# Group-norm chains of a linear-attention and Fourier convolution kernel: four stages on TensorE replaced by two, about a reference mean

## The chip, the cores and the metric

The kernel runs on one core of one Trainium2 chip. The metric is the device time of the whole program in microseconds (us), the median of several executions. The engines are TensorE (PE; its weight loads are listed as PEld), VectorE (DVE), ScalarE (ACT), GpSimd (POOL) and SyncE (SP, which here only issues DMAs). Each takes its instructions in a fixed order; an instruction waits on semaphores for those of other engines and for DMAs.

## What is computed

Two residual layers over an image batch of shape (8, 384, 64, 64), each preceded by a group normalisation over 32 groups of 12 channels:

```python
def _gn(v, G=32, eps=1e-5):
    B_, C_, H_, W_ = v.shape
    g = v.reshape(B_, G, C_ // G, H_, W_)
    m = jnp.mean(g, axis=(2, 3, 4), keepdims=True)
    s = jnp.var(g, axis=(2, 3, 4), keepdims=True)
    return ((g - m) / jnp.sqrt(s + eps)).reshape(v.shape)

x = x + linear_attention(_gn(x), ...)   # 1x1 projections q, k, v, rotary turn, elu+1, output projection
x = x + fourier_conv(_gn(x), ...)       # 1x1 projection, 8x8 block FFT filter, 3x3 depthwise, GELU gate, 1x1 projection
```

## The kernel before

The batch elements b = 0 to 7 are worked one after the other. Channels are three tiles of 128 partitions (`CT = 3`), the 4096 positions are 8 bands of 512 columns (`NBAND`, `BT`). A batch element passes three times: a first pass over its bands makes keys and values (`Keys.project`, lines 455 to 542), a second pass makes queries and adds the attention's output to x (`queries`, lines 1121 to 1181), a third pass does layer 1. The third pass of b is interleaved, band by band, with the first pass of b + 1 (lines 1297 to 1328), and the depthwise sums of b's last two bands are finished inside the second pass of b + 1 (`last_bands`, lines 1244 to 1272).

Everything is issued by one Python program; generators that yield between steps are advanced by hand to set the order on TensorE, and a scheduler of the framework sets the order of the other engines' instructions from the program and its estimates. Tiles come from pools with a fixed number of buffers; the pool "w" has ten, shared by most working tiles.

Statistics. For layer 0 of batch 0, `input_stats` (line 158) runs `bn_stats` on DVE over each band as it lands. For every other normalisation `band_sums` (line 165) accumulates on ACT, band by band, the sum and the sum of squares of each channel about `shift`, minus the mean of the channel's first 64 columns, which DVE makes at band 0 (lines 172 and 173). `mean_and_variance` (line 191) turns either into a mean and a variance for each channel, `mv`.

The chain. `norm_chain` (line 264) takes the channels' `mv` to the groups' mean and inverse deviation and back to the channels. It has four stages on TensorE, each of three `matmul` calls (six instructions in float32):

- `ps_m`: the mean over the group's channels; copied to `gm` (line 291);
- `ps_mc`: that mean sent to the channels; DVE makes each channel's squared difference from it plus its variance, `d` (lines 294 to 298);
- `ps_v`: the mean of `d` over the group; a root on ACT (line 303) and a Newton step on DVE (lines 304 to 310) make `rsg`;
- `ps_r`: `rsg` sent to the channels; `rs` and `nb_` are the scale and the bias of the affine pass `normalised` (line 363, tiles `hf`).

The chain is used nine times: once for layer 0 of batch 0, through `layer0_chain` (line 1020), where `rs` scales the key weights and a third parameter, `shift`, corrects the key bias (`first_k_bias`); and once for layer 1 of each batch, between the second and the third pass. Layer 0 of the batches 1 to 7 uses `far_chain` (line 322) instead, on DVE and POOL's DMAs, inside the second pass. In the layer-1 use the stages stand between other TensorE work: the key projections of the next batch (`pk`, line 490) and the contraction of the last band but one or two (`pw`, lines 946 and 957). How many of these steps come between two stages is set by line 1285:

```python
for steps in (3, 0, 1, 3) if last else (4, 1, 1, 4) if b else (2, 1, 1, 3):
    next(chain)
    for _ in range(steps):
        next(more, None)
run(chain)
```

After the chain come the rest of the key steps, a value projection (`pv`, line 506) and the projection of the first band of layer 1 (`pi`, line 751), which reads `hf`.

The start. As the bands of batch 0 land, TensorE transposes their tokens (`px`, line 452, `turn_tokens`), ACT copies them, DVE takes the statistics; then come the weight sums (`pg_wk`, `pgt_wk`, lines 386 and 391), the chain, the correction of the key bias (`pbk`, line 405), and the key projections.

POOL's queue. In the second pass POOL issues, in this order: the far chain's first two DMAs (lines 329 and 330, `moments`, `of_groups`), the DMAs that add single taps of the depthwise sum to `dw` in place (line 822), the far chain's last four (lines 352 to 358), the bias DMAs (lines 432 and 433), and the outputs (line 978). An instruction that waits there holds all that come after it.

Of the kernel before, what the change touches and what calls it, by code (L numbers as in the profile page):

```python
# [24 lines left out]
NG = 32  # L25
GROUP = C // NG
# [91 lines left out]
def conv_blocks_kernel(ctx: ExitStack, tc: tile.TileContext, a: dict, out: bass.AP, nb: int):  # L118
    nc = tc.nc
# [33 lines left out]
    def line_tile(name):  # L153
        return small.tile([P, C], F32, tag="line", name=name, bufs=1)

    stats, moments = {}, {}

    def input_stats(j):

        if j == 0:  # L160
            stats[0, 0] = w_tile([P, CT, NBAND, 6], "st_0")
        for t in range(CT):
            nc.vector.bn_stats(stats[0, 0][:, t, j, :], xt[0, j][:, t, :])

    def band_sums(b, layer, j, x_, out):


        n = f"{layer}_{b}"
        if j == 0:
            shift = small.tile([P, CT], F32, tag=f"shift{layer}", name=f"shift{n}")  # L170
            sums = small.tile([P, CT, 2, NBAND], F32, tag=f"sums{layer}", name=f"sums{n}", bufs=2 - layer)
            nc.vector.tensor_reduce(shift, x_[:, :, :W], mybir.AxisListType.X, ALU.add)
            nc.vector.tensor_scalar_mul(shift, shift, -1.0 / W)
            moments[b, layer] = shift, sums
        shift, sums = moments[b, layer]
        for m in range(CT):
            of_m = [sums[:, m, i, j : j + 1] for i in range(2)]
            nc.scalar.activation(  # L178
                out[:, m, :], x_[:, m, :], AF.Identity, bias=shift[:, m : m + 1], accum_out=of_m[0]
            )  # L180
            nc.scalar.activation(out[:, m, :], out[:, m, :], AF.Square, accum_out=of_m[1])

    def stream_stats(b, j):

# [3 lines left out]
        nc.sync.dma_start(t, x_in[b][:, :, j * BT : (j + 1) * BT])  # L188
        band_sums(b, 0, j, t, t)

    def mean_and_variance(b, layer):

        mv = small.tile([P, CT, 2], F32, tag="mv", name=f"mv{layer}_{b}")
        if (b, layer) in stats:
            st = stats.pop((b, layer))
            for t in range(CT):
                nc.vector.bn_aggr(mv[:, t, :], st[:, t, :, :].rearrange("p a b -> p (a b)"))
            return mv
# [3 lines left out]
        nc.vector.tensor_scalar_mul(s_[:, :, 0], s_[:, :, 0], 1.0 / N)  # L202
        nc.vector.tensor_sub(mv[:, :, 0], s_[:, :, 0], shift)
        nc.vector.tensor_mul(s_[:, :, 0], s_[:, :, 0], s_[:, :, 0])
        nc.vector.scalar_tensor_tensor(mv[:, :, 1], s_[:, :, 1], 1.0 / N, s_[:, :, 0], ALU.mult, ALU.subtract)
# [29 lines left out]
    def weight(name, queue):  # L235
# [25 lines left out]

    gated = const.tile([P, BT + HT], F32, tag="gated", name="gated")

    def norm_chain(b, layer, params):


        n = f"{layer}_{b}"
        mv = mean_and_variance(b, layer)

        def group_mean(src, name):  # L270
            ps = ps_tile(name)
            for t in range(CT):
                nc.tensor.matmul(
                    ps[:NG, 0:1], to_group[:, t, :], src[:, t : t + 1], start=(t == 0), stop=(t == CT - 1)
                )
            return ps[:NG, 0:1]

        def to_channels(src, name):
            ps = ps_tile(name)
            for m in range(CT):  # L280
                nc.tensor.matmul(
                    ps[:, m : m + 1], of_group[:, m * P : (m + 1) * P], src, start=True, stop=True
                )
            return ps[:, 0:CT]

        def group_tile(name):
            return small.tile([NG, 1], F32, tag=name, name=f"{name}{n}")

        yield
        gm = group_tile("gm")  # L290
        nc.vector.tensor_copy(gm, group_mean(mv[:, :, 0], f"ps_m{n}"))
        yield
        minus_mean = small.tile([P, CT], F32, tag=f"mm{layer}", name=f"mm{n}")
        nc.vector.tensor_scalar_mul(minus_mean, to_channels(gm, f"ps_mc{n}"), -1.0)
        d = small.tile([P, CT], F32, tag="d", name=f"d{n}")
        nc.vector.tensor_add(d, mv[:, :, 0], minus_mean)
        nc.vector.tensor_mul(d, d, d)
        nc.vector.tensor_add(d, d, mv[:, :, 1])
        yield
        var = group_tile("var")  # L300
        nc.vector.tensor_scalar_add(var, group_mean(d, f"ps_v{n}"), 1e-5)
        rsg = group_tile("rsg")
        nc.scalar.activation(rsg, var, AF.Sqrt)
        nc.vector.reciprocal(rsg, rsg)

        y = group_tile("y")
        nc.vector.tensor_mul(y, rsg, rsg)
# [5 lines left out]
        nc.vector.tensor_copy(rs, to_channels(rsg, f"ps_r{n}"))  # L313
        nb_ = small.tile([P, CT], F32, tag=f"nb{layer}", name=f"nb{n}")
        nc.vector.tensor_mul(nb_, minus_mean, rs)
        params += rs, nb_
        if layer == 0:
            shift = group_tile("shift")
            nc.vector.scalar_tensor_tensor(shift, gm, -1.0, rsg, ALU.mult, ALU.mult)
            params.append(shift)  # L320

    def far_chain(b, params):

# [78 lines left out]
    def first_k_bias(params, sums):  # L402

        p_ = ps_tile("pbk_0")
        nc.tensor.matmul(p_[:, :C], params[2].to_broadcast([NG, P]), sums, start=True, stop=True)
# [464 lines left out]
    sums = {}  # L870
# [141 lines left out]
    def layer0_chain(b, prepared):  # L1012

        if b >= nb:
            return
        wk = load_weight(b, "wk", k_runs) if b else first_wk
        params = []
        if b == 0:
            sums = sum_weight(wk, "wk")
            yield from norm_chain(b, 0, params)  # L1020
            scale_weight(wk, params)
            yield
            first_k_bias(params, sums)
            prepared += [params[0], shift_to_all(b, params[2])], wk, kv_bias
# [157 lines left out]

    for j, place in enumerate([None, None, None, "taps", "taps", *ring, None]):
        input_stats(j)
        if j < NBAND - 1:
            transposed[0, j] = xk_tile(0, j, place)
            for i in range(4):
                turn_tokens(0, j, i, transposed[0, j])
# [86 lines left out]
    for b in range(nb):  # L1275
# [136 lines left out]
```

## Time and profile before

| | us |
|---|---|
| median of 3 runs | 3267.61 |
| lowest and highest | 3267.39, 3268.34 |
| the profiled execution | 3267.16 |
| its span on the core | 3265.4 |
| TensorE busy in the span | 3215.4 |
| DVE, ACT, POOL busy | 2622.6, 2155.8, 287.4 |
| first key matmul of batch 0 starts | 32.35 |
| first `pi` of batch 0, 3 and 7 starts | 333.13, 1528.38, 3107.84 |

The profile is one execution, with the start and the duration of each instruction, what ended the idle time before it, and the clock that TensorE was granted. In the views by time a row is: start, duration, engine, line of the kernel, operation, tiles written and read, shapes, count, and in brackets the idle time before it and its releaser. Rows of the same kind in sequence are merged. Matmuls are pipelined, so the time that a group takes from TensorE is read from its start to the start of the next row. A batch's cycle is 398.4 us in the middle of the program.

### The profile page before, as it was taken

The page shows a single profiled execution, that of the slowest core. Times are in us where ns is not written, and L with a number is a line of the kernel's source. Part 1 is how long each engine was busy: PE and PEld are TensorE (multiplying, and loading weights), DVE is VectorE, ACT ScalarE, POOL GpSimd, SP SyncE. Part 2 cuts the span into 40 slices and gives each one's busy share as a digit, 9 for nine tenths or more (in the row PEclk, how much of TensorE's full clock was granted, in tenths as well). Part 3 has the DMA queues.
Part 4 walks back from the last instruction along what each step waited for, and adds up shares of the span by engine and source line. Part 5 has one row for each costly group of instructions (what it writes and reads, how often), then busy time and mean ns, then how long its engine had stood idle before and what let it go on. Part 6 is the DMA issues. An engine that isn't in the chain of part 4 may idle for free.

```text
span 3265.4 us, 53152 instructions
## 1 busy us (share of the span) xinstructions
PE 3215.4 (98%) x21119; PEld 1840.7 (56%) x21119; DVE 2622.6 (80%) x4257; ACT 2155.8 (66%) x4358; POOL 287.4 (9%) x424
## 2 busy tenths in 40 slices
PE   8999999999999999999999999999999999999998
PEld 5544666456664566545665456654566546664455
DVE  6577699886988778896888958988688895988867
ACT  4455666856767566776667766667566674556686
POOL 0000000100001000100001000011000010000065
PEclk9999999999999999999999999999999999999999
DMA  7324243762447524476245652357533573235323
GB/s 221 115 87 112 86 107 99 180 132 86 107 112 175 142 78 100 113 172 150 69 98 134 156 148 66 103 138 153 145 78 98 140 151 99 68 70 131 105 40 59
DMA packets 159484, 377.52 MB, mean 116 GB/s; under 512 B 30372, under 2 KB 41620, under 8 KB 151044
## 3 DMA queue, kind: packets, MB, share of 16 engines
q1 hardware_dynamic: 124500, 282.65, 28.9%
q0 software_dynamic: 34544, 91.26, 17.0%
q8 instruction: 166, 2.72, 0.4%
q14 instruction: 82, 0.67, 0.1%
q10 hardware_dynamic: 192, 0.21, 0.0%
HBM read 235.62 MB, written 99.93 MB: 103 GB/s over the span
## 4 chain that ended last, share of the span: by engine, by line
PE 81%; DVE 10%; ACT 7%; issue 1%; DMA 0%; POOL 0%; SPq 0%; DVEq 0%; ACTq 0%; POOLq 0%
PE pi L751 15%; PE pf L733 14%; PE pk L490 14%; PE pv L506 12%; PE pq L654 8%; PE pw L946 4%; DVE dw L836 4%; PE pd L767 3%; PE pw L957 2%; PE pb L788 2%; PE acc L522 2%; PE acc L535 2%; ACT tap L821 1%; PE pn L692 1%; ACT ring L798 1%
## 5 line engine op out<-in xcount | busy, mean ns | idle before, releaser
L836 DVE SCALAR_TENSOR_TENSOR dw<-ring,w_dw,dw 128x512 f32<-128x512 f32 x1197 | 835.0, 745 | 85.8 <-ACT ring L804 64.8
L490 PE MATMUL pk<-wk,x 128*128 128x384 f32 x1536 | 532.0, 493 | 0.0
L654 PE MATMUL pq<-x,wq 128*128 128x512 f32 x1152 | 512.0, 598 | 11.2 <-DVE qc L666 8.2
L733 PE MATMUL pf<-qc,mt 128*128 128x512 f32 x1152 | 510.2, 596 | 4.5 <-DVE qc L725 4.4
L751 PE MATMUL pi<-w_in,hf 128*128 128x384 f32 x1536 | 506.7, 487 | 4.8 <-ACT ring L798 4.2
L506 PE MATMUL pv<-wv,x 128*128 128x384 f32 x1344 | 461.9, 488 | 0.0
L751 PEld LDWEIGHTS pi<-w_in,hf 128*128 128x128 f32 x1536 | 291.2, 190 | 207.5 <-ACT ring L798 5.0
L490 PEld LDWEIGHTS pk<-wk,x 128*128 128x128 f32 x1536 | 287.6, 191 | 191.5 <-issue 4.5
L733 PEld LDWEIGHTS pf<-qc,mt 128*128 128x128 f32 x1152 | 215.7, 190 | 274.8 <-issue 253.2
L654 PEld LDWEIGHTS pq<-x,wq 128*128 128x128 f32 x1152 | 215.3, 190 | 269.3 <-issue 243.4
L506 PEld LDWEIGHTS pv<-wv,x 128*128 128x128 f32 x1344 | 253.6, 190 | 177.7 <-issue 4.2
L775 DVE TENSOR_TENSOR tf<-pd,filt 128x384 f32<-128x384 f32 x256 | 125.3, 549 | 161.3 <-PE pd L767 161.1
L493 DVE TENSOR_TENSOR kc<-pk,kvbias 128x384 f32<-128x384 f32 x256 | 140.9, 551 | 84.4 <-PE pk L490 84.2
L378 ACT ACTIVATE qs<-qc 128x512 f32<-128x512 f32 (+1 forms) x128 | 106.8, 835 | 148.0 <-DVE qc L683 146.0
L978 POOL DMA_DIRECT2D out_dram<-y x56 | 72.3, 1291 | 1482.0 <-PE pd L767 1046.3
L178 ACT ACTIVATE differences<-x,shift 128x512 f32<-128x512 f32 x192 | 136.9, 713 | 93.6 <-DVE x L737 72.8
L378 ACT ACTIVATE ks<-kc 128x1536 f32<-128x1536 f32 x64 | 95.0, 1484 | 149.8 <-DVE kc L497 149.8
L758 ACT COPY ht<-pi 128x384 f32<-128x384 f32 x256 | 113.4, 477 | 121.0 <-PE pi L751 120.1
L513 ACT COPY v<-pv 128x384 f32<-128x384 f32 x224 | 105.2, 478 | 116.9 <-PE pv L506 114.8
L737 DVE SCALAR_TENSOR_TENSOR x<-pf,bfc,x 128x512 f32<-128x512 f32 x192 | 140.7, 740 | 50.5 <-PE pf L733 49.6
L973 ACT COPY y<-pw 128x512 f32<-128x512 f32 x224 | 90.9, 491 | 128.6 <-PE pw L957 128.6
L946 PE MATMUL pw<-gated,w_out 128*128 128x256 f32 x744 | 172.2, 380 | 0.7 <-DVE tf L775 0.7
(234 smaller groups left out, 4704.2 us busy)
## 6 DMA issues: line engine op xcount, KB each, us to landing
tq<-in_tq SPq DMA_DIRECT2D x64, 1024.0 KB, 7.0
x<-in_x SPq DMA_DIRECT2D x64, 768.0 KB, 4.9
tk<-in_tk SPq DMA_DIRECT2D x64, 768.0 KB, 4.3
out_dram<-x SPq DMA_DIRECT2D x63, 768.0 KB, 6.1
xs<-in_x SPq DMA_DIRECT2D x56, 768.0 KB, 6.2
out_dram<-y POOLq DMA_DIRECT2D x56, 768.0 KB, 8.0
dw<-tap POOLq DMA_DIRECT2D x49, 768.0 KB, 9.8
out_dram<-dw POOLq DMA_DIRECT2D x7, 768.0 KB, 7.5
```

Of the source, the lines that this page charges most:

```text
L178: nc.scalar.activation(out[:, m, :], x_[:, m, :], AF.Identity, bias=shift[:, m : m + 1], accum_out=of_m[0])
L378: nc.scalar.activation(e, x_, AF.Relu, scale=-1.0)
L490: nc.tensor.matmul(pk[:, :C], tokens(t), wks[:, t, :], start=(t == 0), stop=(t == CT - 1))
L493: nc.vector.tensor_add(kc[:, i, :], pk[:, :C], bias)
L506: nc.tensor.matmul(pv[:, :C], xt[b, j][:, t, i * P : (i + 1) * P], wvs[:, t, :], start=(t == 0), stop=(t == CT - 1),)
L654: nc.tensor.matmul(p_, wqs[:, t, m * P : (m + 1) * P], xt[b, j][:, t, :], start=(t == 0), stop=(t == CT - 1),)
L733: nc.tensor.matmul(p_, mt[:, t, m * P : (m + 1) * P], q[:, t, :], start=(t == 0), stop=(t == CT - 1))
L737: latest["sum"] = nc.vector.scalar_tensor_tensor(xm, p_, bfc[:, m : m + 1], xm, ALU.add, ALU.add).ins
L751: nc.tensor.matmul(p_[:, :C], h[:, t, i * P : (i + 1) * P], w_in[:, t, :], start=(t == 0), stop=(t == CT - 1),)
L775: latest["filtered"] = nc.vector.tensor_mul(tf[:, 2 * s + i, :], p_[i][:, :C], filt).ins
L836: latest["tapped"] = nc.vector.scalar_tensor_tensor(acc[:, m], src, wd, acc[:, m], ALU.mult, ALU.add).ins
L946: nc.tensor.matmul(p_[h][:, m - m0, :], w_out[:, 0, m * P : (m + 1) * P], g[:, h * HT : (h + 1) * HT], start=(m == m0), stop=False,)
```

## The change

The moments of a group are taken about a known reference near its mean instead of about the mean itself: each channel gives its mean minus the reference, and its variance plus the square of that difference; the group's averages of both, made in one stage with two columns, give the mean's offset and the variance. One more stage with two columns sends the inverse deviation and minus the offset back to the channels. So `ps_mc` and `ps_v` are gone.

The reference is made ahead of the chain. For layer 0 of batch 0 (`first_reference`) it is the group's mean over the first band: three `bn_aggr`, one stage to the groups, one to the channels, issued directly behind the statistics of band 0. For layer 1 (`of_first_channels`) it is the `shift` of the group's first channel, spread over the group's twelve channels by four DMAs and a copy on POOL's queue, issued when `shift` is made at band 0 of the second pass. The steps between the stages become `(4, 3)` for the batches from 1 on and `(2, 2)` for batch 0.

```diff
@@ band_sums
             nc.vector.tensor_scalar_mul(shift, shift, -1.0 / W)
             moments[b, layer] = shift, sums
+            if layer:
+                of_first_channels(b, shift)
...
+    def of_first_channels(b, shift):
+
+        line = scratch.tile([C], F32, tag="shifts", name=f"shifts_{b}")
+        nc.gpsimd.dma_start(line.rearrange("(t p) -> p t", p=P), shift)
+        at = small.tile([NG, GROUP], F32, tag="by_groups", name=f"by_groups_{b}", bufs=1)
+        nc.gpsimd.dma_start(at, line.rearrange("(g k) -> g k", g=NG))
+        line = scratch.tile([C], F32, tag="references", name=f"references_{b}")
+        nc.gpsimd.tensor_copy(at[:, 1:], at[:, 0:1].to_broadcast([NG, GROUP - 1]))
+        nc.gpsimd.dma_start(line.rearrange("(g k) -> g k", g=NG), at)
+        t = reference[b, 1] = small.tile([P, CT], F32, tag="reference", name=f"reference_{b}", bufs=1)
+        nc.gpsimd.dma_start(t, line.rearrange("(t p) -> p t", p=P))
...
+    def about_reference(b, layer):
+
+        mv, s_, shift = channel_moments(b, layer)
+        ref = reference[b, layer]
+        square = small.tile([P, CT], F32, tag="square", name=f"square{layer}_{b}")
+        if shift is None:
+            nc.vector.tensor_add(mv[:, :, 0], mv[:, :, 0], ref)
+        else:
+            variance(mv, s_)
+            nc.vector.tensor_sub(mv[:, :, 0], s_[:, :, 0], shift)
+            nc.vector.tensor_add(mv[:, :, 0], mv[:, :, 0], ref)
+        nc.vector.tensor_mul(square, mv[:, :, 0], mv[:, :, 0])
+        nc.vector.tensor_add(mv[:, :, 1], mv[:, :, 1], square)
+        return mv, ref
...
+    def first_reference():
+
+        mv = small.tile([P, CT, 2], F32, tag="mv", name="mv_first")
+        for t in range(CT):
+            nc.vector.bn_aggr(mv[:, t, :], stats[0, 0][:, t, 0, :])
+        minus = small.tile([NG, 1], F32, tag="minus", name="minus_first")
+        nc.vector.tensor_scalar_mul(minus, group_means(mv[:, :, 0:1], "ps_first"), -1.0)
+        ref = reference[0, 0] = small.tile([P, CT], F32, tag="reference", name="reference_first", bufs=1)
+        nc.vector.tensor_copy(ref, to_channels(minus, "ps_ref")[:, :, 0])
+        return minus
...
@@ norm_chain
-        mv = mean_and_variance(b, layer)
...
-        yield
-        gm = group_tile("gm")
-        nc.vector.tensor_copy(gm, group_mean(mv[:, :, 0], f"ps_m{n}"))
-        yield
-        minus_mean = small.tile([P, CT], F32, tag=f"mm{layer}", name=f"mm{n}")
-        nc.vector.tensor_scalar_mul(minus_mean, to_channels(gm, f"ps_mc{n}"), -1.0)
-        d = small.tile([P, CT], F32, tag="d", name=f"d{n}")
-        nc.vector.tensor_add(d, mv[:, :, 0], minus_mean)
-        nc.vector.tensor_mul(d, d, d)
-        nc.vector.tensor_add(d, d, mv[:, :, 1])
-        yield
-        var = group_tile("var")
-        nc.vector.tensor_scalar_add(var, group_mean(d, f"ps_v{n}"), 1e-5)
-        rsg = group_tile("rsg")
+        mv, ref = about_reference(b, layer)
...
+        yield
+        both = group_tile("both", 2)
+        rsg, minus = both[:, 0:1], both[:, 1:2]
+        var, y = group_tile("var"), group_tile("y")
+        ps = group_means(mv, f"ps_m{n}")
+        nc.vector.tensor_scalar_mul(minus, ps[:, 0:1], -1.0)
+        nc.vector.tensor_mul(y, minus, minus)
+        nc.vector.scalar_tensor_tensor(var, ps[:, 1:2], 1e-5, y, ALU.add, ALU.subtract)
         nc.scalar.activation(rsg, var, AF.Sqrt)
         nc.vector.reciprocal(rsg, rsg)
...
         yield
         rs = small.tile([P, CT], F32, tag=f"rs{layer}", name=f"rs{n}")
...
         if layer == 0:
             shift = group_tile("shift")
+            nc.vector.scalar_tensor_tensor(shift, minus, first_minus, rsg, ALU.add, ALU.mult)
+            nc.vector.tensor_copy(rs, to_channels(rsg, f"ps_r{n}")[:, :, 0])
+            params += rs, shift
+            return
+        ps = to_channels(both, f"ps_r{n}")
+        nb_ = small.tile([P, CT], F32, tag=f"nb{layer}", name=f"nb{n}")
+        nc.vector.tensor_copy(rs, ps[:, :, 0])
+        nc.vector.tensor_add(nb_, ps[:, :, 1], ref)
+        nc.vector.tensor_mul(nb_, nb_, rs)
+        params += rs, nb_
...
     for j, place in enumerate([None, None, None, "taps", "taps", *ring, None]):
         input_stats(j)
+        if j == 0:
+            first_minus = first_reference()
...
-        for steps in (3, 0, 1, 3) if last else (4, 1, 1, 4) if b else (2, 1, 1, 3):
+        for steps in (4, 3) if last else (4, 3) if b else (2, 2):
             next(chain)
```

`group_means` and `to_channels` are the old inner helpers with as many columns as their source has; `channel_moments` and `variance` are `mean_and_variance` taken apart.

More of the change, by code (lines that the diff above doesn't have):

```diff
@@ L154, in line_tile @@
         return small.tile([P, C], F32, tag="line", name=name, bufs=1)
-    stats, moments = {}, {}
+    stats, moments, reference = {}, {}, {}
     def input_stats(j):
@@ L189, in stream_stats, with channel_moments @@
         band_sums(b, 0, j, t, t)
-    def mean_and_variance(b, layer):
+    def channel_moments(b, layer):
         mv = small.tile([P, CT, 2], F32, tag="mv", name=f"mv{layer}_{b}")
@@ L197, in mean_and_variance @@
                 nc.vector.bn_aggr(mv[:, t, :], st[:, t, :, :].rearrange("p a b -> p (a b)"))
-            return mv
+            return mv, mv[:, :, 0], None
         shift, sums = moments.pop((b, layer))
@@ L202, in mean_and_variance, with variance @@
         nc.vector.tensor_scalar_mul(s_[:, :, 0], s_[:, :, 0], 1.0 / N)
+        return mv, s_, shift
+    def variance(mv, s_):
+        nc.vector.tensor_mul(mv[:, :, 1], s_[:, :, 0], s_[:, :, 0])
+        nc.vector.scalar_tensor_tensor(mv[:, :, 1], s_[:, :, 1], 1.0 / N, mv[:, :, 1], ALU.mult, ALU.subtract)
+    def mean_and_variance(b, layer):
+        mv, s_, shift = channel_moments(b, layer)
         nc.vector.tensor_sub(mv[:, :, 0], s_[:, :, 0], shift)
-        nc.vector.tensor_mul(s_[:, :, 0], s_[:, :, 0], s_[:, :, 0])
-        nc.vector.scalar_tensor_tensor(mv[:, :, 1], s_[:, :, 1], 1.0 / N, s_[:, :, 0], ALU.mult, ALU.subtract)
-        return mv
+        variance(mv, s_)
+        return mv
+    def about_reference(b, layer):
+        mv, s_, shift = channel_moments(b, layer)
+        ref = reference[b, layer]
[3 more added lines that the diff above has]
+        else:
+            variance(mv, s_)
+            nc.vector.tensor_sub(mv[:, :, 0], s_[:, :, 0], shift)
[3 more added lines that the diff above has]
+        return mv, ref
     by_group = const.tile([P, 3 * CT, NG], F32, tag="by_group", name="by_group")
@@ L262, in conv_blocks_kernel, with group_means, to_channels @@
     gated = const.tile([P, BT + HT], F32, tag="gated", name="gated")
+    def group_means(src, name):
+        n = src.shape[-1]
+        ps = ps_tile(name)
+        for t in range(CT):
+            nc.tensor.matmul(ps[:NG, :n], to_group[:, t, :], src[:, t, :], start=(t == 0), stop=(t == CT - 1))
+        return ps[:NG, :n]
+    def to_channels(src, name):
+        n = src.shape[-1]
+        ps = ps_tile(name)
+        for m in range(CT):
+            nc.tensor.matmul(
+                ps[:, n * m : n * m + n], of_group[:, m * P : (m + 1) * P], src, start=True, stop=True
+            )
+        return ps[:, : n * CT].rearrange("p (t i) -> p t i", i=n)
@@ new lines, in first_reference @@
+    def first_reference():
+        mv = small.tile([P, CT, 2], F32, tag="mv", name="mv_first")
+        for t in range(CT):
+            nc.vector.bn_aggr(mv[:, t, :], stats[0, 0][:, t, 0, :])
[4 more added lines that the diff above has]
+        return minus
@@ L264, in norm_chain @@
     def norm_chain(b, layer, params):
         n = f"{layer}_{b}"
-        mv = mean_and_variance(b, layer)
[L270 to L284, printed above, removed]
@@ L286, in group_tile @@
-        def group_tile(name):
-            return small.tile([NG, 1], F32, tag=name, name=f"{name}{n}")
-        yield
-        gm = group_tile("gm")
-        nc.vector.tensor_copy(gm, group_mean(mv[:, :, 0], f"ps_m{n}"))
-        yield
-        minus_mean = small.tile([P, CT], F32, tag=f"mm{layer}", name=f"mm{n}")
-        nc.vector.tensor_scalar_mul(minus_mean, to_channels(gm, f"ps_mc{n}"), -1.0)
-        d = small.tile([P, CT], F32, tag="d", name=f"d{n}")
-        nc.vector.tensor_add(d, mv[:, :, 0], minus_mean)
@@ L297, in norm_chain, with group_tile @@
-        nc.vector.tensor_mul(d, d, d)
-        nc.vector.tensor_add(d, d, mv[:, :, 1])
-        yield
-        var = group_tile("var")
-        nc.vector.tensor_scalar_add(var, group_mean(d, f"ps_v{n}"), 1e-5)
-        rsg = group_tile("rsg")
+        mv, ref = about_reference(b, layer)
+        def group_tile(name, width=1):
+            return small.tile([NG, width], F32, tag=name, name=f"{name}{n}")
+        yield
+        both = group_tile("both", 2)
+        rsg, minus = both[:, 0:1], both[:, 1:2]
@@ L303, in norm_chain @@
+        var, y = group_tile("var"), group_tile("y")
[3 more added lines that the diff above has]
+        nc.vector.scalar_tensor_tensor(var, ps[:, 1:2], 1e-5, y, ALU.add, ALU.subtract)
         nc.scalar.activation(rsg, var, AF.Sqrt)
         nc.vector.reciprocal(rsg, rsg)
-        y = group_tile("y")
         nc.vector.tensor_mul(y, rsg, rsg)
@@ L312, in norm_chain @@
         rs = small.tile([P, CT], F32, tag=f"rs{layer}", name=f"rs{n}")
[L313 to L316, printed above, removed]
         if layer == 0:
             shift = group_tile("shift")
-            nc.vector.scalar_tensor_tensor(shift, gm, -1.0, rsg, ALU.mult, ALU.mult)
-            params.append(shift)
+            nc.vector.scalar_tensor_tensor(shift, minus, first_minus, rsg, ALU.add, ALU.mult)
[8 more added lines that the diff above has]
+        params += rs, nb_
     def far_chain(b, params):
@@ L404, in first_k_bias @@
         p_ = ps_tile("pbk_0")
-        nc.tensor.matmul(p_[:, :C], params[2].to_broadcast([NG, P]), sums, start=True, stop=True)
+        nc.tensor.matmul(p_[:, :C], params[1].to_broadcast([NG, P]), sums, start=True, stop=True)
         nc.vector.tensor_add(kv_bias[:, 0, :], p_[:, :C], kv_bias[:, 0, :])
@@ L1023, in layer0_chain @@
             first_k_bias(params, sums)
-            prepared += [params[0], shift_to_all(b, params[2])], wk, kv_bias
+            prepared += [params[0], shift_to_all(b, params[1])], wk, kv_bias
             return
```

## The prediction

> **What bounds the kernel now.** I read the busy shares first.
>
> ```profile
> PE 3215.4 (98%) x21119; PEld 1840.7 (56%) x21119; DVE 2622.6 (80%) x4257; ACT 2155.8 (66%) x4358; POOL 287.4 (9%) x424
> ```
>
> TensorE (PE) is busy 98% of the span, so a change pays where it takes time out of PE's stream, and costs where it makes PE stand. Second, the list of what PE waited for, in one whole batch (1118 to 1516 us; the three batches beside it that I asked for, from 320 to 1914, show the same three rows):
>
> ```profile
> PE pq L654 <- DVE qc L666: 1.2, 1, 1.2
> PE pb L788 <- DVE qs L666: 0.9, 1, 0.9
> PE pf L733 <- DVE qc L725: 0.6, 1, 0.6
> ```
>
> 2.7 us of waiting in 398, none of it on the normalisation chain. Third, PE in order of time at the end of that batch's layer 0 (start, duration):
>
> ```profile
> 1508.20 0.35 PE L273 MATMUL ps_m<-mv,groups 128*32 128x1 f32 x6
> 1508.48 2.20 PE L490 MATMUL pk<-wk,x 128*128 128x384 f32 x6
> 1510.61 0.82 PE L281 MATMUL ps_mc<-gm,of_group 32*128 32x1 f32 x6
> 1511.37 2.20 PE L490 MATMUL pk<-wk,x 128*128 128x384 f32 x6
> 1513.50 0.35 PE L273 MATMUL ps_v<-d,groups 128*32 128x1 f32 x6
> 1513.78 8.01 PE L490 MATMUL pk<-wk,x 128*128 128x384 f32 x24
> 1521.72 0.82 PE L281 MATMUL ps_r<-rsg,of_group 32*128 32x1 f32 x6
> ...
> 1528.38 7.90 PE L751 MATMUL pi<-w_in,hf 128*128 128x384 f32 x24
> ```
>
> The reader is to see the four stages of the chain: `ps_m` and `ps_v` (sums over groups) take 0.28 us each from their start to the next row's, `ps_mc` and `ps_r` (back to channels) 0.76 and 0.75. Six key matmuls take 2.13 us and twenty-four 7.94, so one takes (7.94 - 2.13)/18 = 0.323 and each break in the run costs 2.13 - 6 x 0.323 = 0.19.
>
> **Six transitions, batches 1 to 6.** Two of the four stages go: 0.28 + 0.76 = 1.04. Two breaks fewer: some 0.3. Two moving columns in place of one I cost at nothing: a group of six is bounded by its weight loads (0.26 of 0.28 us, 0.74 of 0.76, in the rows of the last batch), which stay. Against that, three more DVE operations come ahead of `ps_m`, each 0.20 from start to start (rows L201 to L205, 1506.61 to 1507.45): moments ready at 1508.21, used 0.06 later (as `d` by `ps_v` in the last batch, 3101.53 and 3101.59), against PE's arrival at 1508.20: a wait of 0.07. Gain 1.25 each (bounds 1.0 and 1.35). `ps_r` now stands after the third group of key matmuls, at about 1514.5; its input needs `minus` (1510.15, behind the scaling of `wv`, which waits for its load as before), two operations to `var` (1510.65), the square root (its table load runs 1509.51 to 1510.79), five DVE operations around one key addition: ready at 1512.1. Slack 2.4 us, so no wait. The affine pass `hf` moves ahead of the keys' exponential on ACT, which stood idle 8.21 us there; PE reaches `pi`, its reader, some 9 us later. Sum: -7.5 (-6 to -8).
>
> **The first transition, batch 0.** Here the list of the changed program's instructions, engine by engine, differs: `ps_r` stands directly after the fourth key group, and on DVE the Newton steps that feed it stand behind the keys' turn and sum. DVE at that place before:
>
> ```profile
> 321.97 0.56 DVE L493 TENSOR_TENSOR kc<-pk,kvbias 128x384 f32<-128x384 f32 x1
> ...
> 322.56 0.96 DVE L473 TENSOR_TENSOR ks<-kc,tk 128x768 f32<-128x768 f32 x1
> 323.55 0.96 DVE L481 TENSOR_TENSOR kc<-kc,tk 128x768 f32<-128x768 f32 x1
> 324.43 0.14 DVE L304 RECIPROCAL rsg<-rsg 32x1 f32<-32x1 f32 x1
> ...
> 324.96 0.14 DVE L307 TENSOR_TENSOR y<-rsg 32x1 f32<-32x1 f32 x1
> 325.02 1.74 DVE L497 TENSOR_TENSOR kc<-kc,ks 128x1536 f32<-128x1536 f32 x1
> ```
>
> In the changed order PE gets moments 0.3 us late (eight operations from 315.21 end at 316.80; PE is there at 316.56), does `ps_m` and two key groups, and stands before `ps_r` at 316.86 + 0.28 + 12 x 0.323 + 0.19 = 321.2. DVE then takes: the fourth addition at 321.4 (0.57 to the next), `ks` 321.97 (0.88 to the reciprocal), reciprocal 0.1, `kc` 322.95 (0.87), `y`, the sum L497 from 323.96 (1.67 to the next start), and three operations of 0.18 to 326.1. PE therefore waits 4.9 us (4.4 to 5.3) where before these same DVE rows ran beside three more key groups. Then `ps_r` 0.75, 24 key matmuls 7.94, `pv` 1.93: `pi` starts at 336.8 in place of 333.13, a loss of 3.7. Nothing later takes it back: PE is the bound of the whole loop, and DVE and ACT hang on it.
>
> A gap has a second price, which the trace shows once: 3.05 us of standing at 201.4, and in the microseconds after it (below one of them: busy time of PE, PEld, DVE, ACT, POOL, then PE's granted clock)
>
> ```profile
> 200.54 0.86 PE L692 MATMUL pn<-qc,ks_bd 128*32 128x128 f32 x24
> 204.46 1.86 PE L654 MATMUL pq<-x,wq 128*128 128x512 f32 x3 [3.05 <-ACT mt L569]
> ```
>
> ```profile
> 206.00:207.00 1.00, 1.00 (x3) 0.37 (x2) 1.00 (x4) 0.00 (x0) 0.00 (x0) 0.50 0.00 0
> ```
>
> the granted clock at 0.50 from 205.6 to 209.0; twelve `pq` matmuls took 7.11 us there, against 18 in 7.92 elsewhere, so 1.8 us lost. A longer gap should do no less: I take +1.7, one such stretch, with ends 0 and +3.4 (two; after the start's gaps the clock stayed at 0.50 for 13.7 us). [...] Sum for batch 0: +5.4 (+3.2 to +7.5).
>
> **The last transition.** Before, `ps_v` waited 0.22 and `pi` 0.66 (3107.84). After: `ps_m` behind all twelve `pw` at 3099.55, `var` ready at 3100.45, ACT's table load then follows one diagonal, 3101.15 to 3102.43 (before 3102.39 to 3103.67), `ps_r` at 3103.7, scale and bias ready at 3105.1, `hf` behind seven diagonals and two copies at 3105.7, `pi` 0.86 later at 3106.6. Gain 1.2 (0.5 to 1.5).
>
> **The start.** The last moments are ready at 24.7. The old chain reaches the square root at 28.28 through three PE stages; the new one needs three DVE operations, one PE stage (0.45) and three DVE operations: 26.4, 1.9 earlier. But `first_reference` puts twelve small matmuls at the head of PE's queue, ahead of the transposes: they wait for the first band's statistics (6.00 to 7.88) and three aggregations, and run 0.64 + 1.44 us (the rows of `ps_m` and `ps_mc` at 24.36 and 25.24, slow as here) with a DVE operation between, so the transposes begin at 10.7, not 6.12. Their copies on ACT come every 0.64 us until 10.9 and every 0.40 after; PE in the trace speeds up at 11.0, and after the later start I expect it a stretch of 3.4 us later, at 14.4: 5.8 tiles by then, 22.2 more by 23.2; the weight sums (2.1), their copy and transposes end at 26.2, where before 20.05 led to 23.2. ACT's table load (1.28), behind `by_group`, then allows the root at 27.7. Gain 0.6; PE runs at half clock there until 38.3 in the old trace, which halves it or, if the clock returns a stretch earlier, adds 1.7. I take -0.5 (-2.5 to +1.5).
>
> **POOL and the DMAs.** `of_first_channels` puts four dependent DMAs and a copy per batch on POOL's queue, behind the wait for DVE's shift at 1411.56. Queued behind them are tap 2 of the last band, tap 8 of the one before, taps 3 and 4, then the far chain's four DMAs and the bias lines.
>
> ```profile
> 1376.12 0.80 POOL L329 DMA_DIRECT2D moments<-mv  x1
> 1380.17 0.55 POOL L330 DMA_DIRECT2D of_groups<-moments  x1 [3.25 <-DMA moments<-mv]
> ...
> 1419.71 0.86 POOL L822 DMA_DIRECT2D dw<-tap  x1 [29.90 <-ACT tap L821]
> ```
>
> From `moments` to `of_groups`, issue to issue, is 4.05 us. So: `shifts` 1411.6, `by_groups` 1415.65, landed 3.3 later (0.55 and 2.8), copy 0.2, `references` 1419.1, landed about 4 later, `reference` issue 0.8: POOL is free at 1424 and tap 2 leaves 4.2 us late. The later taps of the same tile follow its landing, and the far chain's DMAs stand behind them, so all move by about 4. First to feel it: DVE's `bias_terms` at 1471.10, whose operand landed at 1455.26 + 5.7 = 1461.0, and the vector taps at 1459.76, whose tile was complete at about 1450. Ten us of slack hide it; cost 0, and with that cover gone a microsecond on DVE, and so on PE, for each beyond. The result is read at 1507. [...]
>
> **Sum.** -0.5 + 5.4 - 7.5 - 1.2 = -3.8 us. The profiled execution took 3267.16 (span 3265.4); it would take 3263.4, and the median of the runs, 3267.61, becomes 3263.8. The ends of the terms sum to -8.8 and +2.5: 3258.8 to 3270.1 for this case alone.
>
> **Rivals.** (1) The gap in batch 0 isn't there, or the clock stays up and the start gains: then eight transitions gain 1.25 and 0.5 comes from the start: -10.5, 3257.1; partly so, -7 to -9. For it: `y` and the reciprocal are tiny and the estimate hangs on one DVE order. Against it: that order is in the program, and DVE's rows there are as good as constant. Chance 0.29. (2) Slower: POOL's hold outlasts the slack. `references` writes to DRAM as `bias_line` does, which left POOL waiting from 1474.01 to 1485.78; 11.8 in place of 4 makes the delay 12, stalls DVE 2 us beyond the slack in seven batches: +14, 3277.8; three such landings give a delay of 28 and over 100. It decides from a delay of about 11.5 on. Against it: the DMA share is 0.00 from 1414 to 1420, where those transfers run. Chance 0.13. (3) My forecast, gains of six transitions half eaten by one gap: 0.58.
>
> A measurement of this kernel can tell about 0.2% (6.5 us) from no change, so faster means under 3261.1 and slower over 3274.1. Range: 3257 to 3272, which leaves out less than half of rival 1's end and most of rival 2. Faster 0.29, same 0.58, slower 0.13.
>
> **What would show it.** Right: a PE wait of 4 to 5 us at `ps_r` on DVE's `both` near 321 and half clock behind it; only `ps_m` and `ps_r` in the later transitions, 18.9 us from `ps_m` to `pi` in place of 20.2; transposes from about 10.7; tap 2 issued some 4 us late and PE's three waits unchanged. Wrong: waits of DVE on DMA at `bias_terms` or the vector taps, no gap in batch 0, or a start that is later than 32.35 for the first key matmul.

## The result, and the profile after

| kernel | median, us (lowest to highest, runs) | median of before beside it | ratio, 95% interval |
|---|---|---|---|
| changed | 3286.91 (3284.78 to 3289.07, 6) | 3267.98 | 1.0058 (1.0045 to 1.0070) |
| changed, measured again with the experiments | 3280.32 (3277.85 to 3281.89, 5) | 3266.49 | 1.0041 (1.0027 to 1.0054) |

The change makes the kernel slower by 0.4 to 0.6%. The forecast was no change, 3263.8 us, with a range up to 3272: wrong in sign and outside the range. The profiled execution of the changed kernel has a span of 3284.6 us (before 3265.4), and its busy shares are

```profile
PE 3210.4 (98%) x21023; PEld 1836.5 (56%) x21023; DVE 2620.4 (80%) x4269; ACT 2156.8 (66%) x4358; POOL 311.1 (9%) x464
```

PE is busy for 5.0 us less than before, and the span is 19.2 us longer: PE stands for 24.2 us more. Of these, 4.87 are a gap in batch 0's transition (shown below). The later transitions are not where the rest is. This is PE in order of time at the end of layer 0 of the batch shown before (start, duration):

```profile
1518.68 0.35 PE L307 MATMUL ps_m<-mv,groups 128*32 128x2 f32 x6
1518.96 6.07 PE L538 MATMUL pk<-wk,x 128*128 128x384 f32 x18
1524.96 0.82 PE L315 MATMUL ps_r<-both,of_group 32*128 32x2 f32 x6
1525.71 9.94 PE L538 MATMUL pk<-wk,x 128*128 128x384 f32 x30
...
1537.43 4.03 PE L799 MATMUL pi<-w_in,hf 128*128 128x384 f32 x12
```

Two stages, no wait in brackets, 18.75 us from `ps_m` to `pi` where the old chain took 20.18: 1.43 gained, and the same in all six such batches. The rest of the loss is in the stretch between two transitions, in the second pass. What PE waited for from 1118.5 to 1518.5 us (total, times, longest):

```profile
PE pq L702 <- DVE qc L714: 1.2, 1, 1.2
PE pb L836 <- DVE qs L714: 0.9, 1, 0.9
PE pf L781 <- DVE qs L714: 0.8, 1, 0.8
PE prb L764 <- DVE parts L756: 0.6, 1, 0.6
PE pf L781 <- DVE qc L773: 0.6, 1, 0.6
PE pq L702 <- DVE x L785: 0.5, 1, 0.5
PE prb L764 <- ACT y L1021: 0.5, 1, 0.5
PE pn L740 <- ACT y L1021: 0.2, 1, 0.2
```

Three of these rows stood in the same view of before. Five are new, each under a microsecond and on other work than the chain: something holds DVE and ACT in the second pass. What holds them begins on POOL, whose rows in order of time are, from the first band's `shift` on (in brackets the idle time before and its releaser):

```profile
1419.24 0.81 POOL L188 DMA_DIRECT2D shifts<-shift  x1 [22.66 <-DVE shift L173]
1429.77 0.55 POOL L190 DMA_DIRECT2D by_groups<-shifts  x1 [9.73 <-DMA shifts<-shift]
1434.72 0.18 POOL L192 COPY by_groups<-by_groups 32x11 f32<-32x11 f32 x1 [4.40 <-DMA by_groups<-shifts]
1435.23 0.51 POOL L193 DMA_DIRECT2D references<-by_groups  x1 [0.33 <-POOL by_groups L192]
1437.09 0.79 POOL L195 DMA_DIRECT2D reference<-references  x1 [1.35 <-DMA references<-by_groups]
1437.88 1.85 POOL L870 DMA_DIRECT2D dw<-tap  x2
1444.19 0.85 POOL L870 DMA_DIRECT2D dw<-tap  x1 [4.47 <-DMA dw<-tap]
```

The queue stands 9.73 us for the landing of `shifts` and 4.40 for that of `by_groups`. The first tap behind them (tap 2 of the last band) goes out at 1437.88, 19.1 us behind L173 (1418.78); before it went out 8.3 behind it (1411.40 to 1419.71). So it is 10.8 us late. Now ACT, then DVE, in order of time in the same stretch:

```profile
1443.68 1.95 ACT L869 ACTIVATE tap<-ring,w_dw 128x512 f32<-128x512 f32 x3 [4.24 <-DMA dw<-tap]
1446.94 0.20 ACT L391 ACTIVATE group_steps<-group_steps 32x1 f32<-32x1 f32 x1
```

```profile
1447.18 0.15 DVE L392 RECIPROCAL group_steps<-group_steps 32x1 f32<-32x1 f32 x1 [4.60 <-ACT group_steps L391]
```

ACT is about to write tap 4 into the tile that tap 2's transfer reads and stands 4.24 us until it has landed. Behind it in ACT's queue is the far chain's square root; DVE's reciprocal waits for that root for 4.60 us with the turn of the queries (`qc`, `qs`) and the sum `x` queued behind it. In the kernel before, ACT ran taps 3 and 4 and then the root without a wait:

```profile
1431.33 2.56 ACT L821 ACTIVATE tap<-ring,w_dw 128x512 f32<-128x512 f32 x4
1435.20 0.20 ACT L343 ACTIVATE group_steps<-group_steps 32x1 f32<-32x1 f32 x1
```

The first of PE's new waits, 0.5 us for `x`, comes at 1449.24, directly behind this. The other four come between 1478 and 1493, where DVE is still behind: its four `qc<-qc,prb` stand at 1468.71, 49.9 us behind L173, and before at 1457.70, 46.3 behind it. That these four descend from the same hold is read, not shown row by row; e3 (below), which lacks the hold, has none of the five. Over the program (total, times, longest):

```profile
ACT tap L869 <- DMA dw<-tap: 34.4, 7, 6.0
```

Before has no such row. The cycles between two `ps_m`, which I read from the trace, say how much it costs (the batch shown above is the third):

```
                first transition to the last, us
before          395.0  398.3  398.3  398.3  398.6  398.3  395.5
changed         404.2  401.7  400.0  401.3  401.3  399.9  397.0
e3 (below)      400.6  396.9  396.9  397.6  396.9  396.9  396.3
```

Two terms that were forecast are seen as forecast. In batch 0:

```profile
312.76 0.32 PE L307 MATMUL ps_m<-mv,groups 128*32 128x2 f32 x6
313.01 4.14 PE L538 MATMUL pk<-wk,x 128*128 128x384 f32 x12
322.02 1.44 PE L315 MATMUL ps_r<-both,of_group 32*128 32x2 f32 x6 [4.87 <-DVE both L354]
...
334.83 7.58 PE L799 MATMUL pi<-w_in,hf 128*128 128x384 f32 x23
```

A wait of 4.87 us, and the granted clock is 0.50 in the view of 320 to 326 us; 22.07 us from `ps_m` to `pi`, before 16.57. And at the start, `px` begins at 10.43, and the first key matmul of batch 0 at 30.02 (before 32.35).

### The profile page after: what moved, and what is told of

It is laid out like the page before. It is cut to its first block, busy times and chain, and to the rows that moved or that the text cites. A ratio compares the mean times of both kernels' runs of the same rounds, so it can differ in the third digit from the quotient of the medians.

```text
span 3284.6 us, 53060 instructions
## 1 busy us (share of the span) xinstructions
PE 3210.4 (98%) x21023; PEld 1836.5 (56%) x21023; DVE 2620.4 (80%) x4269; ACT 2156.8 (66%) x4358; POOL 311.1 (9%) x464
## 4 chain that ended last, share of the span: by engine, by line
PE 64%; DVE 14%; ACT 12%; issue 6%; DMA 4%; POOL 1%; POOLq 0%; DVEq 0%; ACTq 0%; SPq 0%
PE pi L799 15%; PE pk L538 14%; PE pv L554 12%; PE pf L781 6%; DVE dw L884 4%; PE pw L994 4%; PE pd L815 3%; PE pw L1005 2%; PE pb L836 2%; PE acc L570 2%; PE acc L583 2%; DMA dw<-tap 2%; ACT qs L427 2%; ACT qs L426 2%; DVE qc L714 1%
## 5 line engine op out<-in xcount | busy, mean ns | idle before, releaser
L823 DVE TENSOR_TENSOR tf<-pd,filt 128x384 f32<-128x384 f32 x256 | 125.3, 550 | 164.6 <-PE pd L815 164.4
L421 ACT ACTIVATE hf<-x,nb,rs 128x512 f32<-128x512 f32 x192 | 148.1, 808 | 31.0 <-DVE nb L367 30.2
```

What stands on the lines that cost most here:

```text
L421: nc.scalar.activation(dst, src, AF.Identity, bias=nb_[:, t : t + 1], scale=rs[:, t : t + 1])
L823: latest["filtered"] = nc.vector.tensor_mul(tf[:, 2 * s + i, :], p_[i][:, :C], filt).ins
```

## The experiments

The theory is the hold of POOL's queue, with the route just read: the tap's buffer, the root on ACT, DVE's queue, PE. The rivals: the shorter chain costs it itself; the transfers' traffic costs it wherever it lies; the route is the late `inverse`, not the tap. A second theory is that batch 0's gap is a separate loss.

**e1: the old chain with the four transfers.** The kernel before, with `of_first_channels` as in the change, and

```
             moments[b, layer] = shift, sums
+            if layer:
+                of_first_channels(b, shift)
```

> The kernel before, with the four transfers of the group's first channel added behind `shift` and their result used by nothing; the chain keeps its four stages. Theory (the hold): POOL's queue stands behind the landings of `shifts`, `by_groups` and `references` for some 17 to 20 us in each second pass; where taps are in flight (seven cycles) three of their transfers issue about 11 us later, ACT waits some 5 us for a tap's buffer, and PE loses about 4 us a cycle: 3268.0 + 7 * 4 = 3296 us, between 3290 and 3302. In the trace the total of ACT's tap waiting on `dw<-tap` (nothing before, 34.4 us over 7 after) is 25 to 45 us. Rival (the shorter chain itself costs it, by its stages lying closer or by what DVE has to do more): the transfers alone cost nothing, 3268 within 3 us, and no wait on `dw<-tap`.

3288.86 us beside 3267.14 (1.0067, 1.0054 to 1.0080). The transfers alone, their result unused, cost 21.7 us, less than the 28 expected and 1.1 short of the range; ACT's tap waits 28.1 us in seven places. The rival that blames the shorter chain falls.

**e2: the transfers called later.** The call moved from `band_sums` to behind `shift_bc` in `far_chain`.

> The changed kernel, with the same four transfers issued later in POOL's queue: behind `shift_bc` of the far chain (in the last batch at the matching step), so behind the taps and ahead of `bias_line`. Theory (the hold): ACT's tap no longer waits on `dw<-tap` and `group_steps` not on ACT, the seven cycles come back by about 4 us each: 3286.9 - 27 = 3260 us, between 3255 and 3266; `bias_line` and `kvbias` go out some 5 us later, with their slack as cover. Rival (the chain itself, or the transfers' traffic wherever they lie): 3283 to 3290.

3281.23 us (1.0042, 1.0030 to 1.0055). It says nothing on the place: the scheduler set the transfers back ahead of the taps, where `shift` is ready, and POOL's rows have the order of the changed kernel. What it left is a question, since the same queues had measured 3286.91; e13 answers it.

**e3: no transfers from the second batch on.** Any reference near the mean serves, and `ps_r` spreads the group's mean over the channels anyway.

```
-            if layer:
+            if layer and b == 0:
                 of_first_channels(b, shift)
...
-        nc.vector.tensor_add(nb_, ps[:, :, 1], ref)
-        nc.vector.tensor_mul(nb_, nb_, rs)
+        minus_mean = reference[b + 1, 1] = small.tile([P, CT], F32, tag="next", name=f"next_{b}")
+        nc.vector.tensor_add(minus_mean, ps[:, :, 1], ref)
+        nc.vector.tensor_mul(nb_, minus_mean, rs)
```

> The changed kernel with no transfers for layer 1 from the second batch on: the reference of a batch is the group's negated mean that `ps_r` of the batch before has spread over the channels anyway (one tile more, no instruction more); only the first batch, where no taps are in flight, still sends the four. Theory (the hold): 3286.9 - 27 = 3260 us, and a little less than with the transfers later: 3254 to 3263. By the parts read from the two traces: span before 3265.4, start -3.8, first transition +5.5, six later ones and the last -1.4 each, sum 3257.3 of the span, 3259.9 against the median of before. Rival (the chain itself): within 3 us of 3286.9.

3263.87 us beside 3267.14 (0.9988, 0.9979 to 0.9997), 0.9 above the range, whose level rested on 3286.9: 17.4 us under e2, whose queues are those of the changed kernel, in the same set. PE's waits in the batch from 1111 to 1508 us are the three of before again:

```profile
PE pq L703 <- DVE qc L715: 1.2, 1, 1.2
PE pb L837 <- DVE qs L715: 0.9, 1, 0.9
PE pf L782 <- DVE qc L774: 0.6, 1, 0.6
```

and most cycles are 396.9 where before had 398.3 (table above).

**e6: five steps in place of two in the first transition.**

```
-        for steps in (4, 3) if last else (4, 3) if b else (2, 2):
+        for steps in (4, 3) if last else (4, 3) if b else (2, 5):
```

> The changed kernel, with five steps of key projection in place of two between `ps_m` and `ps_r` of the first batch (2, 5 for 2, 2); all else as it was. Theory (batch 0's transition is its own loss, apart from the hold): the wait of 4.87 us at `ps_r` and most of the 6.8 us at half clock go, `ps_m` to `pi` falls from 22.07 us to 15.6 to 17: 3286.9 - 6 = 3281 us, between 3279 and 3283. Rival (the gap only moves to `pi`, which waits for `hf`): `ps_m` to `pi` stays near 20 us and the time within 2 us of 3286.9.

3273.61 us (1.0020, 1.0011 to 1.0029). `ps_m` to `pi` took 14.85 us, less than before's 16.57. The time lies below the range expected, whose level rested on 3286.9; against e2, in the same set, it is 7.6 us, near the 7.4 that the transition gave in the trace (22.27 in e2). The gap did not move to `pi`.

**e2b: the transfers behind `shift_bc`, by an explicit order.**

```
+        latest["spread"] = nc.gpsimd.dma_start(shift_bc, shift.partition_broadcast(P)).ins
+        with tc.issue_after(latest["spread"]):
+            of_first_channels(b - 1, moments[b - 1, 1][0])
```

> The changed kernel, with the four transfers held in POOL's queue behind `shift_bc` by an explicit order (in e2 the scheduler put them back where `shift` is ready, so that their place did not change); only the last batch keeps them where they were. Theory (the hold): the taps' transfers and `inverse` go out as in the kernel before, ACT's tap no longer waits on `dw<-tap`, and the time is that of e3, 3264 us, plus what `bias_line`, then some 5 us later, may cost: 3262 to 3268. Rival (the traffic itself, wherever it lies): 3281 as e2.

3266.15 us (0.9999, 0.9990 to 1.0008), 14 us under the changed kernel of that set. ACT's tap waits once, 3.6 us, in the last batch, where the transfers were left in their place. The traffic is the same as in the changed kernel, at another time, so traffic as such is not the cause.

**e12: behind the four taps, ahead of `inverse`.** `of_first_channels` called behind tap 4's transfer in `last_bands`, `inverse` made to wait for `reference`, and the far chain's last transfers issued three steps later in the program.

```
         add_tap(b, j, 4)
+        with tc.issue_after(latest["tap"]):
+            of_first_channels(b + 1, moments[b + 1, 1][0])
...
+        with tc.issue_after(latest["reference"]):
             nc.gpsimd.dma_start(line.rearrange("(g k) -> g k", g=NG), var)
```

> The changed kernel, with the four transfers behind the transfers of taps 7_2, 6_8, 7_3 and 7_4, and `inverse` behind them, so that the far chain's results are as late as in the changed kernel but the taps are not. Theory (the route is the tap's buffer: `tap` 7_4 on ACT, then the far chain's square root behind it, then DVE's queue): no tap waits on `dw<-tap`, `group_steps` does not wait on ACT, and the time is near e3: 3262 to 3270. Rival (the route is the late `inverse`: `rs`, `shift_bc`, then DVE's `bias_terms`): the time stays at 3278 to 3287.

3263.31 us (0.9989, 0.9981 to 0.9998). POOL in order of time:

```profile
1419.04 0.86 POOL L873 DMA_DIRECT2D dw<-tap  x1 [30.97 <-ACT tap L872]
...
1439.35 1.10 POOL L188 DMA_DIRECT2D shifts<-shift  x1
...
1461.90 0.64 POOL L403 DMA_DIRECT2D inverse<-of_groups  x1
```

With L173 at 1410.71, tap 2 goes out 8.3 us behind it, as before, and `inverse` 51.2 behind it, where the changed kernel has 37.9 and e3 28.8. So an `inverse` later still than in the changed kernel costs nothing, and the taps on time are all that is needed. One thing e12 did not do: `shift_bc` slipped in between and kept its place (43.6 behind L173; 50.8 in the changed kernel). That a late `shift_bc` isn't the route either is read from the changed kernel's own trace alone, where DVE never waits for a transfer at `bias_terms`. The steps from ACT's root over DVE to PE are also read from the trace; no run tests them apart.

**e8: e3 and e6 together.**

> e3 and e6 in one kernel: the reference of the batch before, and five steps in the first transition. If the two losses are apart, they add: e6 took 7.6 us off e2, which stands in POOL's queue as the changed kernel does, so 3263.9 - 7.6 = 3256.3 us, between 3253 and 3259, faster than before by 0.3%. If they overlap: 3259 to 3264.

3255.85 us (3251.62 to 3256.42) beside 3266.49: 0.9965 (0.9953 to 0.9978), the best here, 0.35% under the kernel before and 0.75% under the changed kernel of the same set. The two losses add: against the runs of before beside them, e8 gains 10.6 us and e3 3.3, so 7.4 more, where e6 took 7.6 off e2. The profiled execution is the fastest of the five by 4.1 us and has no stretch at half clock late in the program but the one at its very end, where e3's profile has two more (the mean granted clock is 0.999 in e8 and 0.996 in e3). PE in the first transition, without a wait:

```profile
312.46 0.32 PE L307 MATMUL ps_m<-mv,groups 128*32 128x2 f32 x6
312.71 9.94 PE L539 MATMUL pk<-wk,x 128*128 128x384 f32 x30
322.58 0.82 PE L315 MATMUL ps_r<-both,of_group 32*128 32x2 f32 x6
323.34 2.20 PE L539 MATMUL pk<-wk,x 128*128 128x384 f32 x6
...
327.31 5.00 PE L800 MATMUL pi<-w_in,hf 128*128 128x384 f32 x15
```

**e13: the changed kernel again.** No edit.

> The changed kernel once more, beside the others on one chip, since e2, whose queues stand in the same order, measured 3281.2 us and not 3286.9. If 5.7 us lie between two chips or times, it measures 3279 to 3283 here; if they lie in the program (its lines of DRAM, its place in memory), 3285 to 3289.

3280.32 us: the 5.7 us lie between two sets of runs, not in the program. In the two profiles the first set shows ACT's tap waiting 34.4 us over seven places (26.8 in e13), and two stretches of 3.41 us at half clock, at 1050 and 2252 us, that e13 has not (e13 has one at 3086 that the first has not). Why the landings were longer in the first set is open. Within one set of runs the hold costs 17.4 us by e2 against e3, 17.0 by e13 against e12 and 21.7 by e1 against before; by the first measurement against e3, of another set, it is 23.0.

**Why `shifts` lands so late.** It moves 1.5 KB. Three kernels ask whether it is the queue, the place or the shape of the write. e11 issues the write alone from SP (`nc.sync` for `nc.gpsimd`).

> The changed kernel, with the write of `shifts` alone on SP's queue, the other three as they were on POOL's. If the slow landing belongs to POOL's queue, `shifts` lands in 2 to 4 us and the time falls to 3268 to 3277 us; if it belongs to the scattered 4-byte write, it lands in 8 us or more from SP too, and the time stays at 3278 to 3284, the hold on POOL being the same.

3281.45 us (1.0045, 1.0030 to 1.0060); `shifts` lands in 8.5 us from SP as it does in 8.5 from POOL in e13. It is not the queue. e5 writes each value twice:

```
-        nc.gpsimd.dma_start(line.rearrange("(t p) -> p t", p=P), shift)
+        nc.vector.tensor_copy(twice, shift.unsqueeze(2).to_broadcast([P, CT, 2]))
+        nc.gpsimd.dma_start(line.rearrange("(t p i) -> p t i", p=P, i=2), twice)
...
+        at = pairs[:, :, 0]
```

> The changed kernel, with each value of `shifts` written twice, side by side (384 elements of 8 bytes, as `moments` has, for 384 of 4), so that only the element's size differs; DVE copies one tile more. If writes to DRAM of 4-byte elements are what lands late (`shifts` 8.5 to 9.6 us, `bias_line` some 10, `moments` with 8-byte elements 3.7), `shifts` lands in 3.5 to 4.5 us, POOL stands some 5 us less behind it, and the time is 3268 to 3277 us where the changed kernel has 3280. If it is what goes before it (the store of 768 KB, the stretch of the kernel), `shifts` stays at 8 us or more and the time at 3279 to 3284.

3290.96 us (1.0073, 1.0057 to 1.0090): the time is a miss, the landing a hit. The transfers' rows of e13 and then of e5 (times issued, KB, median us from issue to landing):

```profile
shifts<-shift POOLq DMA_DIRECT2D x8, 1.5 KB, 8.5
by_groups<-shifts POOLq DMA_DIRECT2D x8, 1.5 KB, 5.9
references<-by_groups POOLq DMA_DIRECT2D x8, 1.5 KB, 1.9
```

```profile
shifts<-twice POOLq DMA_DIRECT2D x8, 3.0 KB, 3.6
by_groups<-shifts POOLq DMA_DIRECT2D x8, 3.0 KB, 2.0
references<-by_groups POOLq DMA_DIRECT2D x8, 1.5 KB, 7.8
```

`shifts` falls to 3.6, and `references` rises to 7.8. My edit had made `at` a view with a step of two, so that `references`, until then 32 rows of 48 bytes, went out as 384 single elements. The slow landing followed the scattered 4-byte elements from one transfer to the other, so POOL was held as long as before, and tap 2's transfer also landed some 4 us later than in e13 (ACT's tap waits 38.5 us in all; why that transfer is slower is open). e14 mends this with one whole tile:

```
+        at = small.tile([NG, GROUP], F32, tag="at", name=f"at_{b}", bufs=1)
-        nc.gpsimd.tensor_copy(at[:, 1:], at[:, 0:1].to_broadcast([NG, GROUP - 1]))
+        nc.gpsimd.tensor_copy(at, pairs[:, 0:1, 0].to_broadcast([NG, GROUP]))
```

> e5 once more, with the copy on POOL going into a whole tile of its own, so that `references` is written as 32 rows of 48 bytes again and not as 384 elements of 4 (in e5 it was these that landed late: 7.8 us for 2.1). No transfer writes scattered 4-byte elements now: `shifts` 3.6 us, `by_groups` 2.0, `references` about 2, `reference` issued behind it. Tap 7_2's transfer then goes out some 10 to 11 us behind L173, where e3 has 8.3 and the changed kernel 19.1. The changed kernel's tap waits about 5 us of its 10.8 us of delay, so about 6 us of delay are hidden: theory (a hold of 10 us fits): no wait on `dw<-tap`, 3261 to 3266 us. Rival (any delay of the taps is paid for in part): 3267 to 3275.

3262.59 us beside 3267.08 (0.9985, 0.9976 to 0.9994). The same four transfers, in the same place, on the same queue, at no cost:

```profile
1412.22 0.81 POOL L190 DMA_DIRECT2D shifts<-twice  x1 [23.13 <-DVE twice L189]
1416.12 0.55 POOL L192 DMA_DIRECT2D by_groups<-shifts  x1 [3.09 <-DMA shifts<-twice]
1418.02 0.69 POOL L195 COPY at<-by_groups 32x12 f32<-32x12 f32 x1 [1.35 <-DMA by_groups<-shifts]
...
1421.54 0.79 POOL L198 DMA_DIRECT2D reference<-references  x1 [2.03 <-DMA references<-at]
1422.33 1.85 POOL L873 DMA_DIRECT2D dw<-tap  x2
```

POOL waits 3.09 and 1.35 us for the first two landings where the changed kernel waits 9.73 and 4.40; tap 2 goes out 11.1 us behind L173 (1411.23), 2.8 later than in e3, and no tap waits on `dw<-tap`. A delay of 2.8 us is hidden, one of 10.8 is not.

**e4: all four on SP's queue**, with a transfer that repeats the group's first element in place of POOL's copy.

> The changed kernel, with all four transfers on SP's queue and POOL's copy replaced by a transfer that repeats the group's first element. Theory (it is the hold of POOL's queue, not the transfers, that costs): POOL's taps go out as before, no tap waits on `dw<-tap`; SP's loads and stores stand some 15 us behind the landings, which have tens of us to spare: 3262 to 3268 us. Rival (SP's queue holds a load that is needed sooner): 3270 to 3290, with a new wait on `x<-in_x`, `xs<-in_x` or a weight.

3262.31 us (0.9988, 0.9978 to 0.9997). The transfers are no faster there (`shifts` 8.5 us; `references`, now from repeated single elements, 11.8), and nobody pays: SP's queue had the time.

## Why the prediction was wrong

**The term that failed is POOL's.** The prediction: "POOL is free at 1424 and tap 2 leaves 4.2 us late", and "Ten us of slack hide it; cost 0". Both halves fell. The size: it took the landing from `moments`, 4.05 us from issue to issue; `shifts` took 10.5 (1419.24 to 1429.77), `by_groups` 4.95 where 3.3 was said, and only the copy and `references` were shorter than said (2.4 for 4.2). The tap left 10.8 us late. The row it took has the same number of elements at twice the width: e5 and e14 show that the width is what counts here (`shifts` lands in 3.6 us with 8 bytes in both, in 8.5 with 4 in e13). The nearer row, `bias_line` with its single 4-byte elements and 11.8 us, was read, but used only in the rival, and there for `references`, which is the one write in whole rows. A second such row stood there too: `inverse<-of_groups`, 384 single elements (every second one of a tile), 14.0 us from issue to landing in the batch shown, though right behind a tap's transfer of 768 KB. The slack: it was looked for on DVE, where the result of the delayed transfers is read at last. The first to feel a late transfer was the writer of its source: ACT, which needs tap 2's tile back for tap 4. By e14 and the changed kernel that slack lies between 2.8 us and 10.8; ten was said. In the kernel before, ACT begins tap 4 12.2 us behind the issue of tap 2 (1419.71 to 1431.95, the second of the four operations shown), and in the same batch tap 2's transfer landed in 5.8 us in the changed kernel, 6.3 in e14 and 9.9 in e12. By an estimate from these rows 2.3 to 6.4 us of delay could be hidden, so that even the 4.2 us forecast were not safe. e12 shows that the place where ten were claimed indeed had the room as far as `inverse` and `rs` go.

**The slower rival** had the mechanism (a hold of POOL that outlasts a slack, seven times), the wrong transfer and the wrong victim; its 3277.8 is nearer to 3280.3 and 3286.9 than the forecast. What I set against it, "the DMA share is 0.00 from 1414 to 1420", was no argument: in the changed trace the share is 0.04 in the six microseconds in which `shifts` is waited for (last section): it landed 10.2 us behind its issue with the DMA engines nearly idle.

**The rest of the sum came out near, in part by luck.** With the hold taken away in four ways the kernel measures 3263.9 (e3), 3263.3 (e12), 3262.6 (e14) and 3262.3 us (e4), where -3.8 against the runs of before beside them would give 3262.2 to 3263.3 (e2b, which leaves the hold in the last batch, 3266.2). Term by term: six transitions -1.25 each, measured -1.43. Batch 0 +5.4, measured +5.5 (wait 4.9 said, 4.87 found); e6 and e8 show that it was no price of two stages but of an order, (2, 2). The start -0.5 with -2.5 as its end, measured -2.6 to -4.3 at batch 0's `ps_m`: the clock returned after 3.41 or 6.83 us in place of 13.65, which I had only half counted. The last transition -1.2: `ps_m` to `pi` fell by 1.97 us, but the span from that `ps_m` to the end is unchanged, 166.4 us; a stretch of 3.41 us at half clock stands right behind `pi` at 3125.7, and is worth about 1.7. In e2b, e8 and e12, whose profiles have no such stretch there, the same distance is 164.6 to 164.7, so the gain is there when the clock stays up. The errors offset each other: in e3's profile the start and the six transitions gain some 3.2 us more than was said, batch 0 and the last transition lose 1.8 more, and some 2.6 are lost where the sum had no term, most of it in the last cycle (396.3 us, 394.5 in e8), where a stretch at half clock stands at 3069.6 that e8 has not. The first rival (no gap in batch 0) is out by the row of `ps_r`, though e8 is what it would have been worth.

## What to carry to other kernels

In this kernel, transfers put ahead in a queue were paid for first by the writer of the tile that the next transfer in that queue reads: look for slack at the writer who needs the source back, not only at the reader of what is moved. Price a landing from a row with the same element size, the same side of DRAM and the same traffic ahead of it; here 384 elements of 4 bytes took 8.5 us to be written and 2.5 to be read (`shifts` and `reference` in e13), as many of 8 took 3.6 to be written, and a place behind other transfers made the 8.5 us 14.7 (e12). And before moving a reference value through DRAM, look for one that is already there: the mean of the batch before cost no instruction.

## What the runs showed of the hardware

A write of 384 scattered elements to DRAM landed in 8.5 to 9.6 us (medians) with elements of 4 bytes and in 3.6 with elements of 8, in one place of the program; with 4 bytes it is 8.5 from SP too, and 11.7 and 14.7 where e2b and e12 put it behind other transfers. 32 rows of 48 bytes took 1.6 to 2.6 us. `inverse`, also 384 single elements, took 10.2 to 14.0 right behind a tap's transfer (19.1 in e4) and 7.9 in e12, where none stands right ahead of it. The read behind `shifts` changed with it: `by_groups` took 5.9 us in e13 and 2.0 in e5. The engines aren't moving it all that time. The changed kernel's view by windows, while `shifts` was out (stretch; busy time of PE, PEld, DVE, ACT, POOL; clock, DMA share, GB/s):

```profile
1422.00:1428.00 6.00, 6.00 (x15) 2.66 (x14) 5.07 (x9) 5.94 (x14) 0.00 (x0) 1.00 0.04 3
```

The DMA engines are busy for 4% of six microseconds, and the landing comes at about 1429.5. What passes in between no run here shows.

The clock: after the first gap the programs with the new start show one stretch of 3.41 us at half clock or two, 6.83, and batch 0's `ps_m` comes at 312.3 to 312.8 us with one (the changed kernel, e4, e5, e8) and at 313.3 to 314.0 with two (e2, e2b, e3, e6, e11 to e14). In the changed kernel a wait of 1.27 us at the last `pi` (3125.13) stands just ahead of a stretch of 3.41 us at half clock, at 3125.7; e8 has the same wait, 1.3 us, and no stretch behind it.
